# A grouped 3x3 convolution on normalised images: statistics in groups of 12 images instead of 8, measured further ahead, and 13 of 20 images in the combined form instead of 3 of 5

## The chip, the cores and the metric

The kernel runs on one core of a Trainium2 chip. The core has TensorE (matrix products, PE in the profile), VectorE (DVE), ScalarE (ACT), GpSimd (POOL) and SyncE (SP), which here only issues transfers. Each takes its own instructions strictly in order. They share the on-chip memory SBUF; TensorE writes its sums to a second memory, PSUM, in banks of 512 numbers for each of the 128 partitions. The metric is the time of one execution in microseconds (us); the kernel before takes 968.84 us (median of three).

## The reference, cut to what matters

160 images of 128 channels of 32 x 32 numbers. The output is the input plus a 3x3 convolution of the normalised input. Five sets of weights serve 32 images each.

```python
def _gn(v, G=32, eps=1e-5):                    # group norm: 4 channels of one image
    g = v.reshape(B_, G, C_ // G, H_, W_)
    m = jnp.mean(g, axis=(2, 3, 4), keepdims=True)
    s = jnp.var(g, axis=(2, 3, 4), keepdims=True)
    return ((g - m) / jnp.sqrt(s + eps)).reshape(v.shape)
...
    s1 = (beta - alpha) / RES_DENOS[0]         # beta, alpha: max and min of U
    v1 = s1 * _ste_floor(U / s1)               # the weights in two levels
    s2 = s1 / RES_DENOS[1]
    v2 = s2 * _ste_floor((U - v1) / s2)
    w = (v1 + v2).reshape(OUT_CH * N, IN_CH, K, K)
    xb = x.reshape(B // N, N * C, H, W)
    act = jax.lax.conv_general_dilated(xb, w, ..., feature_group_count=N)
...
x = x + _L0_conv_ref(_gn(x), L0_conv_U)
```

The mean and the variance are taken per image and per four channels, so every image needs two statistics before it can be normalised: the mean and 1 / sqrt(variance + eps).

## The kernel before, in words

**Numbers on TensorE.** A normalised image is split into two 16-bit parts, high and low, and both are multiplied by the weights, which are integers of at most two levels and exact in 16 bits. An image takes one of two forms.

- *Combined* (`combined(i)` true). The convolution is folded over pairs of columns, so that an image needs fewer products. VectorE and GpSimd make four combinations of the raw image as a tile `v` of 2048 numbers per partition (`combine` L681, `outer_columns` L671, `beside_pairs` L698): L687 and L694 on VectorE, L675 and L705 on GpSimd. ScalarE scales `v` by 1 / deviation to the high part `vh` (`high_combined`, L735), and VectorE makes the low part `vl` (`low_combined`, L741). TensorE then does 24 matmuls.
- *Not combined.* The image is normalised to `z` by GpSimd (L711) or, where `by_scalar_too(i)` is true, by ScalarE (`normalise`, L637). ScalarE casts it to `hi` (L645), VectorE makes the low part `lo` (L748) and combines only its rows (`combinations`, L761, L769, L770). TensorE does 30 matmuls, 18 of them on `hi` (`taps`, L785).

Which images are combined: none of the first 7, every odd one up to 29, from 30 to 129 those with `i % 5` of 0, 2 and 4, and from 130 on all but those with `i % 4` of 2.

**Statistics.** Each image is read ahead of time. ScalarE passes over it twice (`measure`): once for the sum (`image_sum`, L241) and once for the squares (`image_square`, L248). Eight early images are measured by VectorE instead (`BY_VECTOR`). Images are put in groups (`self.groups`): small ones up to 24, then 8 images each. When the last image of a group has been measured, the group goes through a chain, one step in each turn of the main loop:

1. `ready`: a small matmul with `gavg` averages the sums over four channels (`means`, L256); at the end of that turn VectorE forms the deviations with `deviations_by_vector` (L296 to L302).
2. `middle`: a second small matmul (`variances`, L273), and ScalarE scales its result to `ve` (`deviation`, L279).
3. `scaled`: GpSimd raises `ve` to the power -1/2 (`power`, L286), and VectorE scales that to `rstd` (L307) and forms `shift`, the mean times `rstd` (`scales_by_vector`, L309).

`shift` is read by ScalarE's `normalise` alone. `by_scalar_too` picks the first seven images and the first image of every group for it.

**The order.** `run` writes out the whole order by hand; no scheduler moves anything. One turn of its loop, for image i, issues in this order: TensorE's sums for image i + 1 and main products of image i (`conv`); VectorE's low part of image i + 2; on GpSimd `power` for a group in step 3, then the combinations or `z` of image i + 4 (both wait for VectorE's last instruction but one, so that they run beside the pairs); ScalarE's sum pass over the image to be measured, then its copy of image i - 1 out of PSUM (`residual`, L926), whose transfer GpSimd issues (`accumulate`, L950, added to the output in memory); ScalarE's copy of a PSUM bank for image i + 1 (`leave`, L888), its high part of image i + 3, and its square pass; on VectorE the start values of image i + 1 (`pairs`, L900 and L902), then `scales_by_vector`, then `combine` of image i + 4, then `deviations_by_vector`. Between these, VectorE and ScalarE make the next set's weights in small steps (`Later`).

**How far ahead.** Turn i measures up to image i + `min(10 + i // 4, STAT_LEAD + 1)` - 1. With `STAT_LEAD` 14 that is 14 ahead from turn 20 on.

**Transfers.** Images come in pairs into 12 buffers of two. SyncE issues a load (L495) once the buffer's former images are used up, by the rule in `consumed(c)`, and four turns later the store of the raw images to the output (L965), to which the copies out of PSUM are added later.

Of the kernel before, what the change touches and what calls it, by code (L numbers as in the profile page):

```python
# [8 lines left out]
F32 = mybir.dt.float32  # L9
I32 = mybir.dt.int32  # L10
MM = mybir.dt.float16
ALU = mybir.AluOpType
# [9 lines left out]
NB = 2  # L22
# [14 lines left out]
class Later:  # L37


    def __init__(self, steps=(), pace=0.0):  # L40
        self.steps = iter(steps)
        self.pace, self.due = pace, 0.0
        self.scalar = False
# [19 lines left out]
    def finish(self):  # L63
        run(self.steps)
# [125 lines left out]
def group_mean_matrix(nc, pool):  # L190

    P = nc.NUM_PARTITIONS
    gavg = pool.tile([P, P // GROUP, GROUP], F32, tag="gavg", name="gavg")
    nc.gpsimd.memset(gavg, 1.0 / GROUP)
    nc.gpsimd.affine_select(
        out=gavg, in_=gavg, compare_op=ALU.is_ge, fill=0.0, base=0,
        pattern=[[-GROUP, P // GROUP], [0, GROUP]], channel_multiplier=1,
    )
    nc.gpsimd.affine_select(
        out=gavg, in_=gavg, compare_op=ALU.is_ge, fill=0.0, base=GROUP - 1,  # L200
        pattern=[[GROUP, P // GROUP], [0, GROUP]], channel_multiplier=-1,
    )
    return gavg.rearrange("p g k -> p (g k)")


class Statistics:
# [5 lines left out]
    def __init__(self, nc, small, gavg, mhalf, nb, scale, name):  # L212
        self.nc, self.small, self.gavg, self.mhalf = nc, small, gavg, mhalf
        self.nb, self.scale, self.name = nb, scale, name
        self.late = False

        self.mv = self.tile("mv", [nb, 2])

# [85 lines left out]
    def scales_by_vector(self):  # L304

        vector = self.nc.vector
        vector.tensor_scalar_mul(self.rstd, self.rstd, self.scale)  # L307
        self.shift = self.tile("shift", [self.nb])
        vector.tensor_tensor(self.shift, self.ngm, self.rstd, ALU.mult)  # L309

    def scales(self):
        nc = self.nc
# [8 lines left out]
def general_path(tc, keep, steps, x, u, out):  # L321
# [8 lines left out]
    with tc.If(far > 0), ExitStack() as ctx:  # L330
# [9 lines left out]
        for n in range(N_SETS):  # L340
            un = one.tile([P, C, TAPS], F32, tag="u", name=f"g_u{n}")
            nc.sync.dma_start(un, uv[n])
            wn = one.tile([P, C, TAPS], F32, tag="w", name=f"g_w{n}")
            k1, k2 = run(steps.quantise(one, un, f"g{n}", F32))
            nc.vector.tensor_scalar_mul(wn, k1, steps.s1)
            nc.vector.scalar_tensor_tensor(wn, k2, steps.s2, wn, ALU.mult, ALU.add)
# [38 lines left out]
class Main:  # L385
# [21 lines left out]

    STAT_LEAD = 14  # L410
    LOAD_LEAD = 18
    CHUNKS = 12
    STEADY = 7
# [3 lines left out]
    EARLY = 8  # L417
    FIRST = 3
    HURRIED = (0, 2, 4, 8, 24)


    COLS = (1, 0, 2)
# [3 lines left out]
    def __init__(self, tc, ctx, keep, x, u, out):  # L426
        self.tc = tc
        nc = self.nc = tc.nc
        self.imgs, C, self.H, self.W = x.shape
        P = self.P = nc.NUM_PARTITIONS  # L430
        assert C == P and self.H * self.W == 1024
        self.per_set = self.imgs // N_SETS
        self.xv = x.rearrange("(b n) c h w -> n c b (h w)", n=N_SETS)
        self.ov = out.rearrange("(b n) c h w -> n c b (h w)", n=N_SETS)
        self.uv = u.rearrange("n (o i k) -> n o i k", o=C, k=TAPS)

        def pool(name, bufs, **kw):
            return ctx.enter_context(tc.tile_pool(name=name, bufs=bufs, **kw))

        self.const = pool("const", 1)  # L440
        self.qpool = pool("quant", 1)
        self.wpool = pool("weights", 2)
        self.upool = pool("u", 1)
        self.xpool = pool("x", self.CHUNKS)
        self.zpool = pool("z", 2)
        self.parts = pool("parts", 4)
        self.rows = pool("rows", 4)
        self.wide = pool("wide", 2)
        self.wide_parts = pool("wide_parts", 3)
        self.evac = pool("evac", 2)  # L450
        self.sums = pool("sums", 3)
        self.unread = pool("unread", 1)
        self.small = pool("small", 3)
        self.ps_eo = pool("ps_eo", 2, space=PSUM)
        ps_m = pool("ps_m", 1, space=PSUM)
        ps_small = pool("ps_small", 1, space=PSUM)
        self.steps = Steps(nc, keep)

        self.m1a, self.m1b, self.m2_ps = (
            ps_m.tile([P, self.H // 2, self.W], F32, tag=name, name=name)  # L460
            for name in ("m1a", "m1b", "m2")
        )
        self.pair = [self.m1a, self.m2_ps]

        small = ps_small.tile([P, 512], F32, tag="small", name="small")
        self.pt, self.pg = small[:, : ROW * P].rearrange("p (k o) -> p k o", k=ROW), small[:, ROW * P :]
        self.chunks, self.z, self.hi, self.v, self.eo, self.m2 = {}, {}, {}, {}, {}, {}
        self.sum, self.stored = {}, {}
        self.tables, self.wts, self.across = {}, {}, {}
        self.columns = []  # L470

        cuts = [0, 2, 4, 8, 12, 16, 20, *range(24, self.imgs + 1, 8)]
        self.groups = [range(a, b) for a, b in zip(cuts, cuts[1:])]
        self.group_of = {i: k for k, g in enumerate(self.groups) for i in g}
        self.stats = {}
# [117 lines left out]
    def keep_sums(self, n, col):  # L593
        wt = self.wts[n, col]
        run(self.both_sums(
            self.nc.gpsimd, wt[:, self.SUM], wt[:, self.DIFF], *(wt[:, k] for k in range(ROW))
        ))
# [9 lines left out]
    def stats_of(self, k):  # L607
        if k not in self.stats:
            self.stats[k] = Statistics(
                self.nc, self.small, self.gavg, self.mhalf, len(self.groups[k]),  # L610
                self.steps.lift, k,
            )
            self.stats[k].late = self.groups[k].start not in self.HURRIED
        return self.stats[k]

    def measure(self, i, stages=(0, 1)):
# [31 lines left out]
    def combined(self, i):  # L648

        if i < self.STEADY or i >= self.imgs:  # L650
            return False

        if i < self.FIFTHS:
            return i % 2 == 1
        return i % 5 % 2 == 0 if i < self.THIRDS else i % 4 != 2

    def by_scalar_too(self, i):

        return i < self.FIRST + 4 or i == self.groups[self.group_of[i]].start

    def column_of(self, i):

# [306 lines left out]

    def consumed(self, c):  # L970

        return max(i + 2 if self.by_hand(i) else i - 2 for i in range(c * NB, c * NB + NB))

    def run(self):
        nc, P = self.nc, self.P
# [26 lines left out]
        self.ident5 = self.const.tile([P, P], MM, tag="ident5", name="ident5")  # L1002
        nc.gpsimd.tensor_scalar_mul(self.ident5, ident, 5.0)
        self.gavg = group_mean_matrix(nc, self.const)
        self.mhalf = self.const.tile([P, 8], F32, tag="mhalf", name="mhalf")
        nc.gpsimd.memset(self.mhalf, -0.5)

        self.los = []
# [97 lines left out]
        for i in range(self.imgs):  # L1106
# [30 lines left out]
            else:  # L1137
                j = i - 1
                self.conv(i, on_the_way)
            ahead = i + min(10 + i // 4, self.STAT_LEAD + 1)  # L1140
            to_measure = range(measured, min(self.imgs, ahead))
# [163 lines left out]
```

## Time and profile before

| | |
|---|---|
| runs, us | 968.79, 968.84, 969.57; median 968.84 |
| profiled execution, us | 968.17 |
| its span, first to last instruction, us | 966.4 |
| TensorE clock granted | 0.998 of full |
| PE busy | 926.9 us, 96% of the span |
| VectorE busy | 910.1 us, 94% |
| ScalarE busy | 862.0 us, 89% |
| GpSimd busy | 463.6 us, 48% |
| transfers | 254.22 MB, 263 GB/s mean |

The profile shows one execution. The span is what the instructions cover; about 1.8 us lie around it, so a change of the span is a change of the profiled execution's time, and the median of the runs stands 0.67 us above that one. Lines such as L735 are lines of the kernel before. In a group of instructions the name left of the arrow is written and the names right of it are read. An instruction's duration on ScalarE or VectorE overlaps the next one by up to 0.1 us, and a matmul's by more, so that time per instruction is better read from one start to the next. After an idle stretch the profile names in brackets what ended it. The kernel's first 60 us hold the first weights; the turns of the loop after that take 4.7 to 8.4 us each.

### The profile page before, as it was taken

How to read it: one execution, taken by the hardware profiler on the slowest of the kernel's cores; microseconds unless marked ns; L12 is line 12 of the kernel's file. 1: busy time of each engine (PE TensorE's matmuls, PEld its weight loads, DVE VectorE, ACT ScalarE, POOL GpSimd, SP SyncE). 2: the span in 40 equal slices, each digit the busy share in tenths (PEclk: the TensorE clock that was granted, in tenths of full speed). 3: DMA queues.
4: the chain of work that ended last, by engine and by line, in shares of the span. 5: the costliest groups of instructions: out<-in, count | busy, mean ns of one | idle time of the engine just before them, and what ended most of it. 6: DMA issues, size and time to landing. Idle time of an engine off the chain costs nothing.

```text
span 966.4 us, 13055 instructions
## 1 busy us (share of the span) xinstructions
PE 926.9 (96%) x4432; PEld 433.6 (45%) x4432; DVE 910.1 (94%) x1280; ACT 862.0 (89%) x1167; POOL 463.6 (48%) x477
## 2 busy tenths in 40 slices
PE   2999999999999999999999999999999999999997
PEld 1444444444444444444444444444444444444443
DVE  7999999999999999989999999999999998998995
ACT  5879999999999999999989999999989999998561
POOL 4345344446445444554355435534445545666550
PEclk9999999999999999999999999999999999999999
DMA  9079999999999999999999999999999999666663
GB/s 363 20 273 340 338 328 321 334 322 315 327 320 328 314 327 323 311 315 258 283 243 287 276 305 286 278 251 301 278 274 260 286 275 255 98 90 107 91 107 112
DMA packets 67450, 254.22 MB, mean 263 GB/s; under 512 B 5296, under 2 KB 5296, under 8 KB 67376
## 3 DMA queue, kind: packets, MB, share of 16 engines
q1 hardware_dynamic: 45344, 173.09, 47.6%
q0 software_dynamic: 22032, 80.23, 44.7%
q8 instruction: 36, 0.59, 0.2%
q14 instruction: 38, 0.31, 0.1%
HBM read 89.19 MB, written 164.10 MB: 262 GB/s over the span
## 4 chain that ended last, share of the span: by engine, by line


## 5 line engine op out<-in xcount | busy, mean ns | idle before, releaser
L785 PE MATMUL eo<-hi,wt 128*128 128x496 f16 (+3 forms) x1170 | 310.3, 375 | 0.9 <-ACT wt L567 0.9
L840 PEld LDWEIGHTS <-wt 128*128 128x128 f16 x1884 | 183.9, 99 | 211.5 <-DVE rows L770 1.7
L741 DVE SCALAR_TENSOR_TENSOR vl<-v,rstd,vh 128x2048 f16<-128x2048 f32 x94 | 221.5, 2356 | 1.0 <-ACT vh L735 0.9
L840 PE MATMUL eo<-vh,wt 128*128 128x512 f16 x561 | 210.2, 375 | 0.2 <-DVE eo L902 0.2
L840 PE MATMUL eo<-vl,wt 128*128 128x512 f16 x561 | 210.1, 375 | 0.0
L735 ACT ACTIVATE vh<-v,rstd 128x2048 f16<-128x2048 f32 x94 | 188.1, 2001 | 13.4 <-DVE v L694 13.0
L926 ACT COPY sum<-eo 128x1024 f32<-128x1024 f32 x153 | 160.7, 1050 | 29.4 <-PE eo L840 28.5
L675 POOL TENSOR_SCALAR v<-xt,ngm 128x64 f32<-128x64 f32 x94 | 83.0, 883 | 215.5 <-issue 66.8
L785 PEld LDWEIGHTS <-wt 128*128 128x128 f16 x1242 | 120.9, 99 | 140.2 <-DVE eo L902 2.6
L248 ACT ACTIVATE junk<-xt,mv 128x1024 uint8<-128x1024 f32 x152 | 174.4, 1147 | 0.1
L840 PEld LDWEIGHTS <-across 128*128 128x128 f16 x1128 | 110.3, 98 | 140.3 <-issue 13.3
L241 ACT ACTIVATE junk<-xt 128x1024 uint8<-128x1024 f32 x152 | 160.5, 1056 | 13.8 <-DMA xt<-in_x_dram 10.7
L711 POOL TENSOR_SCALAR z<-xt,ngm,rstd 128x1024 f32<-128x1024 f32 x49 | 90.5, 1847 | 155.9 <-DVE rows L769 45.9
L840 PE MATMUL eo<-rows,wt 128*128 128x512 f16 x378 | 143.5, 380 | 0.0
L950 POOL DMA_DIRECT2D out_dram<-sum x153 | 133.8, 876 | 9.5 <-ACT sum L926 6.1
L840 PE MATMUL m<-vl,across 128*128 128x496 f16 (+1 forms) x282 | 105.6, 374 | 9.5 <-DVE vl L741 9.5
L687 DVE TENSOR_TENSOR v<-xt 128x960 f32<-128x960 f32 x94 | 109.0, 1160 | 0.0
L840 PE MATMUL m<-vh,across 128*128 128x496 f16 (+1 forms) x282 | 105.6, 375 | 0.9 <-ACT m L888 0.9
L888 ACT ACTIVATE m<-m 128x512 f32<-128x512 f32 x157 | 93.8, 597 | 13.4 <-PE m L840 13.2
L705 POOL TENSOR_TENSOR v<-xt 128x512 f32<-128x512 f32 x94 | 97.2, 1034 | 0.0
L748 DVE TENSOR_TENSOR lo<-z,hi 128x1024 f16<-128x1024 f32 x66 | 80.6, 1220 | 0.0
L286 POOL TENSOR_TENSOR rstd<-ve,mhalf 128x8 f32<-128x8 f32 (+2 forms) x24 | 39.1, 1629 | 68.8 <-DVE rows L769 22.0
(150 smaller groups left out, 1182.3 us busy)
## 6 DMA issues: line engine op xcount, KB each, us to landing
xt<-in_x_dram SPq DMA_DIRECT2D x78, 1024.0 KB, 12.7
out_dram<-sum POOLq DMA_DIRECT2D x153, 512.0 KB, 8.8
out_dram<-xt SPq DMA_DIRECT2D x76, 1024.0 KB, 18.6
out_dram<-xt SPq DMA_DIRECT2D x7, 512.0 KB, 3.7
u<-in_L_conv_U_dram SPq DMA_DIRECT2D x4, 576.0 KB, 19.0
xt<-in_x_dram SPq DMA_DIRECT2D x4, 512.0 KB, 9.7
range<-in_L_conv_U_dram SPq DMA_DIRECT2D x3, 576.0 KB, 7.9
u<-in_L_conv_U_dram SPq DMA_DIRECT2D x2, 288.0 KB, 3.2
```

Of the source, the lines that this page charges most:

```text
L241: self.nc.scalar.activation(junk, image, ACTF.Copy, scale=-1.0 / image.shape[1], accum_out=self.mv[:, j, 0:1],)
L248: self.nc.scalar.activation(junk, image, ACTF.Square, bias=self.mv[:, j, 0:1], accum_out=self.mv[:, j, 1:2],)
L687: nc.vector.tensor_tensor(self.view(v, 1, (511, 2), (half, H), (1, half - 1)), self.view(x, 1, (1, 2), (W, H), (2, half - 1)), self.view(x ...
L705: ins = nc.gpsimd.tensor_sub(self.v[i][:, 1536:], odd, even)
L711: ins = nc.gpsimd.tensor_scalar(z, self.image(i), st.ngm[:, j], st.rstd[:, j], ALU.add, ALU.mult)
L735: self.nc.scalar.mul(vh, self.v[i], st.rstd[:, j])
L741: yield self.nc.vector.scalar_tensor_tensor(vl, self.v[i], st.rstd[:, j], self.hi[i], ALU.mult, ALU.subtract)
L785: nc.tensor.matmul(self.bank(target, a)[:, first:end, c0:c1], self.wts[n, col][:, k, :], tile[:, s0 : s0 + 2 * (end - first) - 1 : 2, c0 + ...
L840: self.nc.tensor.matmul(out, weights, moving, start=start and j == 0, stop=False, skip_group_check=True)
L888: self.nc.scalar.mul(m2, self.m2_ps, 0.5)
L926: nc.scalar.copy(self.as_banks(i, self.sum[i]), self.flat(i, eo))
L950: added = self.nc.gpsimd.dma_start(self.ov[n, :, b], self.sum.pop(i), accum_op=ALU.add)
```

## The change

Four things.

- Groups: 8 images each up to 48, then 12 each up to 144, then two of 8. Twenty groups instead of twenty-four. The constant tile `mhalf` grows from 8 to 16 columns. `STAT_LEAD` becomes 19, so that the distance grows up to 19 images, reached at turn 40; the two agree up to turn 23. Counted from its first image, a group of 12 goes through its chain one turn earlier than a group of 8 did, and the last two groups, of 8, five turns earlier.
- `shift`: groups that start at 32 or later have none, and no image from 32 on is normalised by ScalarE; the first image of a group goes to GpSimd like the others.
- Which images are combined from 30 to 129: those with `i * 13 % 20 < 13`, 65 instead of 60.
- `consumed`: a buffer counts as used up one turn earlier.

```diff
@@ class Statistics
-        self.late = False
+        self.late = self.shifted = False
@@ def scales_by_vector
         vector.tensor_scalar_mul(self.rstd, self.rstd, self.scale)
-        self.shift = self.tile("shift", [self.nb])
-        vector.tensor_tensor(self.shift, self.ngm, self.rstd, ALU.mult)
+        if self.shifted:
+            self.shift = self.tile("shift", [self.nb])
+            vector.tensor_tensor(self.shift, self.ngm, self.rstd, ALU.mult)
@@ class Main
-    STAT_LEAD = 14
+    STAT_LEAD = 19
...
+    BY_SCALAR = 32
@@ def __init__
-        cuts = [0, 2, 4, 8, 12, 16, 20, *range(24, self.imgs + 1, 8)]
+        cuts = [0, 2, 4, 8, 12, 16, 20, 24, 32, 40, *range(48, self.imgs - 12, 12), 152, self.imgs]
@@ def stats_of
             self.stats[k].late = self.groups[k].start not in self.HURRIED
+            self.stats[k].shifted = self.groups[k].start < self.BY_SCALAR
@@ def combined
-        return i % 5 % 2 == 0 if i < self.THIRDS else i % 4 != 2
+        return i * 13 % 20 < 13 if i < self.THIRDS else i % 4 != 2
@@ def by_scalar_too
-        return i < self.FIRST + 4 or i == self.groups[self.group_of[i]].start
+        start = self.groups[self.group_of[i]].start
+        return i < self.FIRST + 4 or i == start and start < self.BY_SCALAR
@@ def consumed
-        return max(i + 2 if self.by_hand(i) else i - 2 for i in range(c * NB, c * NB + NB))
+        return max(i + 2 if self.by_hand(i) else i - 3 for i in range(c * NB, c * NB + NB))
@@ def run
-        self.mhalf = self.const.tile([P, 8], F32, tag="mhalf", name="mhalf")
+        self.mhalf = self.const.tile([P, 16], F32, tag="mhalf", name="mhalf")
```

## The prediction

> **What bounds the kernel now.** I read the page's first part, then the table of windows, the waits, and two stretches of the timeline. (The page's chain that ended last is empty here.) I call one turn of the image loop in `run` pass i.
>
> ```profile
> PE 926.9 (96%) x4432; PEld 433.6 (45%) x4432; DVE 910.1 (94%) x1280; ACT 862.0 (89%) x1167; POOL 463.6 (48%) x477
> ```
>
> Three engines stand near the span, so a mean says little. By stage (columns: PE, weight load, DVE, ACT, POOL busy us, clock, DMA share, GB/s):
>
> ```profile
> 187.00:303.00 116.00, 115.65 (x558) 54.46 (x558) 111.52 (x155) 111.62 (x154) 57.96 (x57) 1.00 1.04 320
> 303.00:412.00 109.00, 108.82 (x523) 50.95 (x522) 106.35 (x150) 106.02 (x143) 50.96 (x51) 1.00 1.04 322
> 412.00:785.00 373.00, 368.44 (x1767) 172.07 (x1766) 358.17 (x492) 354.76 (x486) 176.68 (x174) 1.00 1.01 278
> 785.00:945.00 160.00, 157.10 (x748) 73.27 (x747) 147.58 (x175) 132.95 (x160) 92.64 (x81) 1.00 0.72 136
> ```
>
> From 187 us on TensorE all but never stops; ScalarE and VectorE follow at 95 to 96% until 785. The matmuls' ends are modelled, so I checked by start times: a matmul starts every 0.21 us without a break, except in a few places. From the waits, the reason for nearly all of those:
>
> ```profile
> PE m L840 <- DVE vl L741: 9.5, 9, 1.9
> DVE rstd L307 <- POOL rstd L286: 2.9, 13, 0.2
> ```
>
> The timeline shows one of the two largest, at the moment when a group's scales are made:
>
> ```profile
> 489.54 1.84 POOL L286 TENSOR_TENSOR rstd<-ve,mhalf 128x8 f32<-128x8 f32 x1 [4.09 <-DVE rows L770]
> 490.50 0.70 DVE L902 SCALAR_TENSOR_TENSOR eo<-m1b,m 128x512 f32<-128x512 f32 x1
> 491.42 0.36 DVE L307 TENSOR_SCALAR rstd<-rstd,lift 128x8 f32<-128x8 f32 x1 [0.22 <-POOL rstd L286]
> 491.72 1.03 POOL L705 TENSOR_TENSOR v<-xt 128x512 f32<-128x512 f32 x1
> 491.82 0.97 DVE L309 TENSOR_TENSOR shift<-ngm,rstd 128x8 f32<-128x8 f32 x1
> 492.70 1.15 DVE L687 TENSOR_TENSOR v<-xt 128x960 f32<-128x960 f32 x1
> 494.61 2.00 ACT L735 ACTIVATE vh<-v,rstd 128x2048 f16<-128x2048 f32 x1 [1.93 <-DVE v L694]
> 496.83 0.38 PE L840 MATMUL m<-vl,across 128*128 128x512 f16 x1 [1.94 <-DVE vl L741]
> ```
>
> An 8-column `shift` takes 0.97 us because it ends with POOL's L705; the combination L687 is late, then `vh`, then `vl`, then TensorE. By start times TensorE loses 2.11 us here, 2.11 at 725, 1.13 at each of 816, 860 and 904, 0.84 at 466, 0.35 at 409, and crumbs: 9.1 us after 303. Before that, the last loss is ScalarE's:
>
> ```profile
> 186.68 0.62 ACT L888 ACTIVATE m<-m 128x512 f32<-128x512 f32 x1
> 187.35 0.38 PE L840 MATMUL m<-vh,across 128*128 128x512 f16 x1 [0.94 <-ACT m L888]
> ```
>
> At 187 us, in pass 24, ScalarE has no lead at all over TensorE. The new lead begins to differ in this very pass.
>
> **The Trainium skill.** "SBUF — State Buffer", section "Who interferes with whom": a VectorE instruction with two SBUF inputs contends with a GpSimd instruction that reads SBUF, and whoever starts first blocks the other. The trace agrees: `shift` takes 0.16 us alone and 0.96 beside L705, and L687 lies over L705 by more than 0.1 us only where it is itself longer. "TensorE: Matmul & The Clock Gate", "Back-to-back issue gap": it gives 216 ns for an isolated 512-column matmul and 131 ns in a stream; the trace has 0.215 us in the stream, so I use the trace. "Perfetto Trace Analysis", "Identifying the Most-Contended Engine": occupancy measures VectorE and ScalarE fairly, matmul busy time does not; hence the start times.
>
> **Five more combined images.** From 30 to 129, 65 instead of 60 are combined. A combined image has 24 matmuls: 12 go from 837.99 to 840.53, so 5.08 us. Another has 30: 1.30 (404.70 to 406.00) plus 5.10 (840.53 to 845.77 less a 0.14 statistics matmul), 6.39. TensorE saves 5 x 1.31 = 6.5 us, and it is the bound. ScalarE pays 1.90 instead of 0.94 each (start to start), +4.8. VectorE pays 2.26 + 1.07 + 0.66 = 3.99 for 1.13 + 0.60 + 2 x 0.34 = 2.41, +7.9 in all. POOL gains five pairs L675/L705, +9.6; its 49 images of L711 stay 49, since five group starts move to it.
>
> **Groups of 12.** 24 groups become 20. TensorE: 4 x 2 x 0.14 = -1.1 us. VectorE: four times 0.53 for the means and 0.27 for `rstd`, -3.2. ScalarE: five `z` of group starts, 5 x 1.27 = -6.4. The power takes 0.8 us for 2 columns, about 1.1 for 4, 1.76 for 8: for 12 I estimate 2.4, between 1.8 (all fixed) and 2.6 (in proportion). VectorE already waits for it, so +0.6 in each of eight moments.
>
> **No shift.** The row gives 16 x 0.53 = 8.5 us. I count almost nothing: where it took 0.96, L687, also with two SBUF inputs, waits in its place until L705 is over. Bounds: -0.9 and 0 us in each moment.
>
> **Where the moments fall.** Scales are made in the pass that also combines the image four ahead. Before, that was pass start - 4 and the group's first image; now it is start - 5 and image start - 1 (image 38 for the group at 40, 139 and 147 for the last two). Before, all five stalls of over 1 us came at starts 80, 120, 136, 144 and 152, the second of two combined images in a row; 40 is the one such start without a stall. Where the image stood otherwise (32, 64, 72, 104, 112) TensorE lost at most 0.35, and five starts are not combined. Now only 31 and 71 are second; 47, 59, 107, 119, 131, 139 and 147 are first in their row, 38, 83 and 95 not combined. With the longer power I take 2.7 us for 72, 0.6 for each of 48, 60, 108, 120, 132, 144 and 152, and 0.8 as at 466: 7.7 instead of 9.1. Bounds 4 (all first ones are free) and 12 (VectorE, with 3 to 4 us more work and less TensorE time to hide it, stalls at all).
>
> **Measuring further ahead.** Passes 24, 28, 32, 36 and 40 measure two images: five early pairs of 1.04 + 0.21 + 0.96 + 0.09 = 2.30 us on ScalarE, 11.5, paid back only after pass 140, where ScalarE has room anyway. ScalarE's instructions of passes 24 to 43, start to start: 20 x (0.96 + 0.48 + 2.30) = 74.8; `vh` and `hi` of images 27 to 46: 12 x 1.90 + 8 x 0.94 = 30.3; weights and small things 2.8; together 107.9, against 112.3 between the copies of images 24 (186.7) and 44 (299.0). New: 74.8 + 11.5 + 13 x 1.90 + 7 x 0.94 + 2.8 = 120.4. With no lead at 187 the copy of image 44 comes at 307.1, and TensorE, 0.6 behind, begins the sums of image 45 at 307.7 instead of 303.2: +4.5, and 0.5 for ScalarE's own waits, +5.0. Bounds +1 (the copies get ahead in ways the sum doesn't see) and +10. What is queued behind the extra pair is `sum`, then `m`, for which VectorE's L900 and then TensorE wait.
>
> Transfers must stay hidden for that:
>
> ```profile
> xt<-in_x_dram SPq DMA_DIRECT2D x6, 1024.0 KB, 30.5
> out_dram<-sum POOLq DMA_DIRECT2D x11, 512.0 KB, 8.7
> ```
>
> That is 187 to 245 us. The load of images 46 and 47 starts at 186.7, lands at 217.3 and is read at 233.9. Read in pass 30 it has about 8 us of cover instead of 16.6, images 54 and 55 about 4. The load's earlier place (`consumed`) helps little here, since SP's queue stands some 10 us behind in this stage (the load that pass 21 asks for, over at about 177, starts at 186.7), held by stores of inputs that have not landed yet; at worst it delays one store. I count 0, up to 4 if a landing slips. The wider `mhalf` is set once in the prologue: 0.
>
> **Sum.** TensorE after pass 44: of the 6.5, 1.3 lie inside the ramp, where ScalarE decides; -5.2. Statistics matmuls -1.1. Stalls 7.7 - 9.1 = -1.4. Ramp +5.0. Together -2.7 on 968.17 (profiled execution: span 966.4 and 1.8 around it): 965.5. The median of the runs lies 0.67 above it, so 966.1.
>
> **Rivals.**
> Full gain: the ramp costs 0.5. For it: VectorE had 1.41 us of idle at 242 and ScalarE 1.19 at 218, so the stage has some give. Against: ScalarE's lead of zero at 187. 966.1 - 4.5 = 961.6.
>
> Wash: VectorE becomes the second bound and stalls come to 10 or more. For it: while weights are made its instructions fill 97 to 99% of TensorE's time. 968.8.
>
> Slower: ScalarE stays the limit from pass 24 to 64 with waits of its own. Its instructions there come to 229.1 us; with 3% of waits (before it had 4% in passes 24 to 43) 236.2, against 225.4 before, +10.8. Only three images and three groups are saved after that, -4.7, and 1.5 of stalls: +4.6, 973.4. It decides once the ramp costs over 7.7 us. Against it: as the laggard it rarely waits for the others.
>
> Inert: the instruction lists have the 30 and 8 fewer matmuls, so that is excluded.
>
> **Numbers.** About 0.2%, 1.9 us, is what a measurement can tell from no change. The forecast has 0.53 (own range 963 to 969.5, of it 0.36 faster, 0.15 same, 0.02 slower), full gain 0.17, wash 0.14 (0.12 same, 0.02 slower), slower 0.16. Faster 0.53, same 0.27, slower 0.20. Range 960.5 to 972.5.
>
> **What would show it.** Right: copy of image 44 near 307, ScalarE's busy share near full from 187 to there, TensorE waiting for L888; from there the same images closer together; stalls on `vl` fewer, with L687 lengthened beside L705. Wrong: L241 waiting for a load, no wait for L888 in the ramp, or VectorE's stalls rising beyond 500 us.

## The result and the profile after

The changed kernel takes 976.18 us (median of four, 975.57 to 977.07) against 968.97 us for the kernel before beside it: a ratio of 1.0077, with a 95% interval of 1.0065 to 1.0089. It is 0.8% slower, where 966.1 us was forecast. Its profiled execution took 977.07 us with a span of 975.3, so the span grew by 8.9 us. The granted clock is 0.996 against 0.998. The lines of the changed kernel that follow L309 have numbers higher by one to four: L844 is what was L840, L745 what was L741, L892 what was L888.

The page's first part, after:

```profile
PE 923.8 (95%) x4386; PEld 427.5 (44%) x4386; DVE 910.6 (93%) x1235; ACT 862.8 (88%) x1158; POOL 478.9 (49%) x483
```

Every engine but GpSimd is busy as long as before to within 1 us, or shorter, and still the span is longer. So the change bought its work and lost more in waiting. Where, the table of windows shows (PE, weight load, DVE, ACT, POOL busy us, clock, DMA share, GB/s):

```profile
187.00:303.00 116.00, 109.01 (x521) 50.46 (x521) 107.12 (x146) 115.18 (x161) 55.28 (x54) 1.00 1.04 327
303.00:412.00 109.00, 104.58 (x496) 47.64 (x495) 104.68 (x135) 103.77 (x143) 51.73 (x52) 1.00 1.03 296
412.00:785.00 373.00, 364.80 (x1728) 168.06 (x1727) 358.14 (x466) 353.87 (x475) 188.98 (x177) 1.00 0.99 275
785.00:945.00 160.00, 160.00 (x763) 74.63 (x761) 146.44 (x169) 127.87 (x151) 95.32 (x84) 1.00 0.75 149
```

From 187 to 303 us TensorE now starts 521 matmuls where it started 558, and ScalarE has become full: 115.18 of 116. From 303 to 785 TensorE is idle more often too. Only in the last row is it better than before: it no longer stops at all. The waits, after:

```profile
PE m L844 <- DVE vl L745: 12.1, 15, 2.0
PE m L844 <- ACT m L892: 6.6, 6, 1.7
PE m L844 <- DVE rows L774: 2.8, 7, 0.8
DVE rstd L307 <- POOL rstd L286: 5.5, 8, 0.9
```

There are thus two new losses: ScalarE's in the ramp, as I call the stretch from 187 to 303 us, where the distance grows (6.6 where it was 0.9), and more of VectorE's `vl` (12.1 where it was 9.5, although the tail's three are gone).

**A ledger by start times.** As in the prediction I count what TensorE loses between the start of one matmul and the next, beyond the 0.21 us that it takes in a stream. TensorE's own work fell by 6.5 + 1.1 = 7.6 us by the prediction's counts; the losses after 187 us came to 9.0 before and 24.0 after. Together +7.4, where the spans of the two profiled executions differ by 8.9 and the medians by 7.2. The trace shows what the ledger leaves out of the spans. From 455.6 to 458.9 us the changed kernel's matmuls start 0.42 us apart instead of 0.21, eight times in a row, although TensorE waits for nothing. That is 1.6 us more. The table of windows has a granted clock of 0.59 around it, where the longer stretches above have 1.00:

```profile
454.80:459.00 4.20, 4.11 (x12) 1.56 (x12) 4.17 (x6) 4.17 (x7) 2.24 (x3) 0.59 0.93 264
```

With that the ledger has +9.0 for the 8.9. The kernel before has no such stretch in its profiled execution but in the first 30 us and the last 6, nor has e8, which is the changed kernel but for `shift`; so nothing ties these 1.6 us to the change. Why the clock fell there the record doesn't show.

The same ledger for each kernel that was run (us lost in each stretch; the median and the ratio to the kernel before beside it). It leaves out stretches at half the clock (e9 has one at 361 us as well; e4, e5, e6 and e9 have one near 41 us), and one stall of 1.1 us, ending between 187 and 189 us, that every kernel has:

| kernel | 187-303 | 303-785 | 785-945 | span | median | ratio (95%) |
|---|---|---|---|---|---|---|
| before | 0 | 5.6 | 3.4 | 966.4 | 968.97 | 1 |
| after | 7.5 | 16.5 | 0 | 975.3 | 976.18 | 1.0077 (1.0065-1.0089) |
| e1, before with 13 of 20 | 2.2 | 17.3 | 3.4 | 974.6 | 977.73 | 1.0097 (1.008-1.0113) |
| e2, after with 3 of 5 | 5.2 | 7.4 | 0 | 968.9 | 970.72 | 1.0024 (1.0014-1.0034) |
| e3, after with groups of 8 | 3.9 | 12.6 | 0 | 966.9 | 969.55 | 1.001 (1.0003-1.0017) |
| e4, after, five images unmeasured | 1.0 | 15.1 | 0 | 967.1 | 968.88 | 1.0003 (0.9994-1.0012) |
| e5, after, no scales made from 48 | 7.6 | 4.7 | 0 | 962.4 | 964.31 | 0.9955 (0.9938-0.9971) |
| e6, after, half of `vl` | 7.5 | 2.9 | 0 | 961.0 | 962.66 | 0.9934 (0.9918-0.9951) |
| e7, after, groups of 8 and 3 of 5 | 1.2 | 2.3 | 0 | 961.0 | 963.35 | 0.9947 (0.993-0.9963) |
| e8, after with all shifts | 7.5 | 17.3 | 0.3 | 974.6 | 976.83 | 1.0086 (1.0069-1.0103) |
| e9, e7 with 65 combined, spread | 5.2 | 18.5 | 0 | 976.5 | 978.29 | 1.0087 (1.0069-1.0105) |
| e10, e7 with 60 in the new order | 3.1 | 9.2 | 0 | 970.2 | 971.52 | 1.0022 (1.0013-1.003) |
| e11, before with distance 15 | 1.2 | 3.6 | 0.2 | 961.9 | 964.09 | 0.9948 (0.9932-0.9965) |

The kernel before took 968.87 us beside e1 to e4, 968.42 beside e5 to e8, and 969.29 beside e9 to e11.

**The ramp, in the timeline of the changed kernel.** ScalarE and the TensorE instruction that waits for it:

```profile
249.68 1.14 ACT L248 ACTIVATE junk<-xt,mv 128x1024 uint8<-128x1024 f32 x1
...
250.81 0.17 ACT L279 ACTIVATE ve<-small 128x8 f32<-128x8 f32 x1
250.87 0.83 ACT L134 ACTIVATE nnn<-u,s1r 128x384 int16<-128x384 f32 x1
251.60 1.05 ACT L241 ACTIVATE junk<-xt 128x1024 uint8<-128x1024 f32 x1
...
252.64 1.06 ACT L930 COPY sum<-eo 128x1024 f32<-128x1024 f32 x1
253.59 0.59 ACT L892 ACTIVATE m<-m 128x512 f32<-128x512 f32 x1
...
254.23 0.38 PE L844 MATMUL m<-vh,across 128*128 128x512 f16 x1 [1.61 <-ACT m L892]
```

ScalarE has no gap, none of its instructions carries a bracket, and TensorE waits 1.61 us for the bank that L892 empties. It is one of the six waits of that row; the others end at 188 (the one that every kernel has), 200, 235, 273 and 290 us.

**A moment, in the same kernel.** A moment is the place in VectorE's order where a group's scales are made (L307). This is the group of 96, whose scales are made beside an image that is not combined. VectorE, GpSimd's two instructions, and TensorE:

```profile
584.56 2.34 DVE L745 SCALAR_TENSOR_TENSOR vl<-v,rstd,vh 128x2048 f16<-128x2048 f32 x1
...
584.80 4.27 POOL L286 TENSOR_TENSOR rstd<-ve,mhalf 128x12 f32<-128x12 f32 x1 [1.15 <-DVE v L698]
...
589.08 1.18 POOL L715 TENSOR_SCALAR z<-xt,ngm,rstd 128x1024 f32<-128x1024 f32 x1
589.10 1.19 DVE L307 TENSOR_SCALAR rstd<-rstd,lift 128x12 f32<-128x12 f32 x1 [0.85 <-POOL rstd L286]
...
590.20 2.34 DVE L745 SCALAR_TENSOR_TENSOR vl<-v,rstd,vh 128x2048 f16<-128x2048 f32 x1
...
600.17 0.82 PE L844 MATMUL m<-rows,wt 128*128 128x512 f16 x3 [0.22 <-DVE rows L774]
...
603.10 2.35 DVE L745 SCALAR_TENSOR_TENSOR vl<-v,rstd,vh 128x2048 f16<-128x2048 f32 x1
...
605.50 0.38 PE L844 MATMUL m<-vl,across 128*128 128x512 f16 x1 [1.05 <-DVE vl L745]
```

VectorE loses 0.85 us waiting and 1.10 in L307, 1.95 together. Between 590.20 and 605.36 it has no idle of as much as 0.1 us: each instruction follows the one ahead. The delay comes out at TensorE 11 and 16 us later, as 0.38 and 1.21 us by start times. A stall and its cause do not lie in the same pass; only the row of uninterrupted VectorE instructions between them joins them.

### The profile page after: what moved, and what is told of

Read it like the earlier page. It is cut to its first block, busy times and chain, and to the rows that moved or that the text cites. A ratio compares the mean times of both kernels' runs of the same rounds, so it can differ in the third digit from the quotient of the medians.

```text
span 975.3 us, 12918 instructions
## 1 busy us (share of the span) xinstructions
PE 923.8 (95%) x4386; PEld 427.5 (44%) x4386; DVE 910.6 (93%) x1235; ACT 862.8 (88%) x1158; POOL 478.9 (49%) x483
## 4 chain that ended last, share of the span: by engine, by line
## 5 line engine op out<-in xcount | busy, mean ns | idle before, releaser
L789 PE MATMUL eo<-hi,wt 128*128 128x496 f16 (+3 forms) x1080 | 286.4, 375 | 0.7 <-ACT wt L569 0.7
L844 PEld LDWEIGHTS <-wt 128*128 128x128 f16 x1884 | 182.7, 99 | 217.1 <-DVE rows L774 6.7
L745 DVE SCALAR_TENSOR_TENSOR vl<-v,rstd,vh 128x2048 f16<-128x2048 f32 x99 | 232.1, 2345 | 1.1 <-ACT vh L739 0.9
L844 PE MATMUL eo<-vh,wt 128*128 128x496 f16 (+1 forms) x591 | 221.4, 375 | 1.2 <-DVE eo L906 1.2
L844 PE MATMUL eo<-vl,wt 128*128 128x496 f16 (+1 forms) x591 | 221.3, 375 | 0.0
L739 ACT ACTIVATE vh<-v,rstd 128x2048 f16<-128x2048 f32 x99 | 198.1, 2001 | 15.7 <-DVE v L698 15.4
L844 PEld LDWEIGHTS <-across 128*128 128x128 f16 x1188 | 116.5, 98 | 158.3 <-issue 26.6
L241 ACT ACTIVATE junk<-xt 128x1024 uint8<-128x1024 f32 x152 | 160.5, 1056 | 14.5 <-DMA xt<-in_x_dram 11.1
L715 POOL TENSOR_SCALAR z<-xt,ngm,rstd 128x1024 f32<-128x1024 f32 x49 | 104.6, 2134 | 132.9 <-DVE rows L774 26.2
L789 PEld LDWEIGHTS <-wt 128*128 128x128 f16 x1152 | 111.9, 99 | 130.7 <-DVE eo L906 3.8
L844 PE MATMUL eo<-rows,wt 128*128 128x512 f16 x348 | 132.1, 380 | 0.0
L844 PE MATMUL m<-vl,across 128*128 128x496 f16 (+1 forms) x297 | 111.5, 376 | 12.1 <-DVE vl L745 12.1
L691 DVE TENSOR_TENSOR v<-xt 128x960 f32<-128x960 f32 x99 | 119.2, 1204 | 0.0
L844 PE MATMUL m<-vh,across 128*128 128x496 f16 (+1 forms) x297 | 111.5, 375 | 6.6 <-ACT m L892 6.6
L892 ACT ACTIVATE m<-m 128x512 f32<-128x512 f32 x157 | 94.1, 599 | 14.7 <-PE m L844 14.5
L698 DVE SCALAR_TENSOR_TENSOR v<-xt,twice 128x512 f32<-128x512 f32 x99 | 73.7, 745 | 0.0
```

The costliest lines, as they stand in the source:

```text
L241: self.nc.scalar.activation(junk, image, ACTF.Copy, scale=-1.0 / image.shape[1], accum_out=self.mv[:, j, 0:1],)
L691: nc.vector.tensor_tensor(self.view(v, 1, (511, 2), (half, H), (1, half - 1)), self.view(x, 1, (1, 2), (W, H), (2, half - 1)), self.view(x ...
L715: ins = nc.gpsimd.tensor_scalar(z, self.image(i), st.ngm[:, j], st.rstd[:, j], ALU.add, ALU.mult)
L739: self.nc.scalar.mul(vh, self.v[i], st.rstd[:, j])
L745: yield self.nc.vector.scalar_tensor_tensor(vl, self.v[i], st.rstd[:, j], self.hi[i], ALU.mult, ALU.subtract)
L789: nc.tensor.matmul(self.bank(target, a)[:, first:end, c0:c1], self.wts[n, col][:, k, :], tile[:, s0 : s0 + 2 * (end - first) - 1 : 2, c0 + ...
```

## The experiments

**One part at a time.** The pattern alone on the kernel before, the pattern undone in the changed kernel, and the groups undone there.

```diff
# e1_pattern_only (kernel before)
-        return i % 5 % 2 == 0 if i < self.THIRDS else i % 4 != 2
+        return i * 13 % 20 < 13 if i < self.THIRDS else i % 4 != 2
```

> The kernel before with one part of the change: 13 of 20 images combined from 30 to 129; groups of 8, the lead of 14, shift and the buffers' rule stay. TensorE has 6.5 us less to do. Theory A (the loss is ScalarE's ramp in passes 24 to 43, about 6 us, and little else): the saving shows, 963 to 965 us. Theory B1 (VectorE can't carry five more combined images while weights are made): stalls on vl eat it, 968 to 971. Theory B2 (VectorE is held up by the longer power of groups of 12 and its place): as A, 963 to 965.

Measured: 977.73 us, 8.9 above the kernel before and above all that was expected; B1, with stalls on `vl`, came nearest. The ledger has most of the price: TensorE did 6.5 us less work, and lost 22.9 us instead of 9.0, all but some 2 us of it to `vl`.

```diff
# e2_pattern_undone (changed kernel)
-        return i * 13 % 20 < 13 if i < self.THIRDS else i % 4 != 2
+        return i % 5 % 2 == 0 if i < self.THIRDS else i % 4 != 2
```

> The changed kernel with 3 of 5 images combined from 30 to 129, as before; groups of 12, the lead of 19 and no shift stay. TensorE's work is that of before less 1.1 us, the ramp costs ScalarE the same 11.5 us. A: ramp +6, stalls as before: 974. B1: the same, 974, since VectorE has its old load. B2: the moments of the scales go on costing, TensorE stalls after 303 us of about 16 us instead of 9: 980.

Measured: 970.72 us, 5.5 less than the changed kernel. The pattern costs 5.5 us in this setting, on top of its 6.5 us less work. Losses after 187 us are halved, 24.0 to 12.6. All three theories expected more, 974 to 980.

```diff
# e3_groups_of_8 (changed kernel)
-    STAT_LEAD = 19
+    STAT_LEAD = 15
-        cuts = [0, 2, 4, 8, 12, 16, 20, 24, 32, 40, *range(48, self.imgs - 12, 12), 152, self.imgs]
+        cuts = [0, 2, 4, 8, 12, 16, 20, *range(24, self.imgs + 1, 8)]
```

> The changed kernel with groups of 8 images from 24 on and a lead of 15 instead of 19 (so that the scales are still made at start - 5); 13 of 20 combined and no shift stay. One early pair of passes on ScalarE instead of five. A: ramp cost 1 to 1.5 instead of 6, the rest saved: 964. B1: VectorE's stalls stay at about 16 us: 970 to 972. B2: power back to 1.8 us per group, stalls back to 9: 964.

Measured: 969.55 us, 6.6 less than the changed kernel. With a distance of 15 a group has its scales five turns ahead of its first image, as the groups from 48 to 132 have in the changed kernel. So groups of 12 with their longer distance cost 6.6 us here. The ledger has 3.6 of it in the ramp and 3.9 after 303, less 1.1 for the statistics matmuls. A and B2 had 964; B1's 970 to 972 came nearest.

**The ramp.** GpSimd writes constants in place of ScalarE's two passes over images 39, 44, 49, 54 and 59, those that the growing distance adds.

```diff
# e4_five_unmeasured (changed kernel)
+    UNMEASURED = (39, 44, 49, 54, 59)
+        if i in self.UNMEASURED:
+            for s in stages:
+                self.nc.gpsimd.memset(st.mv[:, j, s : s + 1], (0.0, 1024.0)[s])
+            return
```

> The changed kernel with the two ScalarE passes of images 39, 44, 49, 54 and 59 left out (GpSimd writes constants in place of their sums, so these five images and their groups are normalised with other numbers); all else stays. ScalarE has in passes 24 to 43 what it had before. A: the ramp's cost goes, 6 to 7.5 us less than the changed kernel: 969 to 970. B1 and B2: the same for this stage, with TensorE's stalls after 303 us still at 16. If ScalarE's ramp is not the limit: 976.

Measured: 968.88 us, 7.3 less than the changed kernel. Of the six waits for ScalarE's copy only the one is left that every kernel has, and the ramp's losses fall from 7.5 to 1.0; after 303 us they are nearly what they were (15.1 for 16.5). The cause of the ramp's loss is shown: five pairs of ScalarE's passes, put ahead where ScalarE has nothing to spare.

**The stalls of the main stretch.** Two kernels take away one side each: the moments (from the group of 48 on, constants stand for the scales, so neither the power nor L307 is done), or VectorE's load (it makes half of `vl`, and TensorE reads that half twice).

```diff
# e5_no_moments (changed kernel)
             self.stats[k].late = self.groups[k].start not in self.HURRIED
+            self.stats[k].fixed = self.groups[k].start >= 48
...
+        if self.fixed:      # in power
+            return self.nc.gpsimd.memset(self.rstd, 2.0**14 * 0.0023)
...
+        if self.fixed:      # in scales_by_vector
+            return
```

> The changed kernel in which groups that start at 48 or later take a constant scale: GpSimd writes it in place of the power, and VectorE's instruction on rstd is left out (so images from 48 on are scaled by a fixed number). The ten moments after 48 cost VectorE and GpSimd next to nothing; all other work stays. Theory C (each moment holds VectorE up by 1.5 to 2.3 us, and with 13 of 20 combined VectorE has no slack to make it good, so TensorE pays): stalls after 303 us fall from 16.5 to about 3, 962 to 964 us. Theory B1 (VectorE simply has too much work with five more combined images, moments or not): stalls stay above 10, 971 or more.

```diff
# e6_half_low (changed kernel)
+        w = 1024 if i >= self.FIFTHS else 2048
-            vl, self.v[i], st.rstd[:, j], self.hi[i], ALU.mult, ALU.subtract
+            vl[:, :w], self.v[i][:, :w], st.rstd[:, j], self.hi[i][:, :w], ALU.mult, ALU.subtract
...
-            source = source[:, quarter * 512 : quarter * 512 + 512]
+            q = quarter % 2 if j == 1 and i >= self.FIFTHS else quarter
+            source = source[:, q * 512 : q * 512 + 512]
```

> The changed kernel in which VectorE makes only half of vl (1024 of 2048 columns) for combined images from 30 on, and TensorE reads that half twice, so that the low part of these images is wrong for two of four combinations. VectorE has about 1.1 us less per combined image; TensorE, ScalarE, GpSimd and the moments keep all their work. Theory C and theory B1: with slack on VectorE the delays are made good, stalls on vl after 303 us nearly vanish, the ramp stays: 961 to 964. If the moments reach TensorE whatever VectorE's slack is: 974 to 976.

Measured: 964.31 and 962.66 us, 11.9 and 13.5 less than the changed kernel. The waits of TensorE for `vl`, first in e5 (where L750 is the `vl`), then in e6 (L746):

```profile
PE m L849 <- DVE vl L750: 4.7, 7, 1.4
```

```profile
PE m L846 <- DVE vl L746: 2.8, 3, 1.4
```

Both kernels do the full changed pattern on TensorE with the full ramp (7.6 and 7.5 us lost from 187 to 303). Without moments the losses from 303 to 785 fall from 16.5 to 4.7; with VectorE relieved, and every moment in its place, to 2.9. So it takes both: a moment costs TensorE something only because VectorE has nothing to spare, and VectorE's fullness costs little without moments. The moment of 84 shows it in e6: VectorE waits 0.85 us for the power and spends 1.10 in L307, as in the changed kernel, and TensorE loses nothing in the 20 us after it, where it lost 1.6. In e5 the stalls of 72, 84, 96, 108 and 120 are gone and 60's as well; of those around the moment of 48 one of 1.22 us stays, at 320 us, and one of 0.87 at 371, which thus need no moment from 48 on.

**The shift, and a combination of the rest.**

```diff
# e8_shift_kept (changed kernel)
-            self.stats[k].shifted = self.groups[k].start < self.BY_SCALAR
+            self.stats[k].shifted = True
```

> The changed kernel with shift still made for every group, though nobody reads it from 32 on. If taking shift away only moved its wait to the next instruction with two SBUF inputs, as the prediction says: 976 to 977. If the whole time of shift was saved (12 moments at 0.5 to 0.97 us, passed on to TensorE): 982 to 987.

Measured: 976.83 us against 976.18: no difference that the intervals tell apart. Leaving out the shift is worth nothing that these runs can show.

```diff
# e7_groups_8_pattern_old (changed kernel)
-    STAT_LEAD = 19
+    STAT_LEAD = 15
-        cuts = [0, 2, 4, 8, 12, 16, 20, 24, 32, 40, *range(48, self.imgs - 12, 12), 152, self.imgs]
+        cuts = [0, 2, 4, 8, 12, 16, 20, *range(24, self.imgs + 1, 8)]
-        return i * 13 % 20 < 13 if i < self.THIRDS else i % 4 != 2
+        return i % 5 % 2 == 0 if i < self.THIRDS else i % 4 != 2
```

> The changed kernel with groups of 8, a lead of 15 and 3 of 5 images combined: of the change only the missing shift, the group starts on GpSimd, the scales one pass earlier and the buffers' rule stay. TensorE's work is that of before. One early pair of passes costs 1 to 2 us. Theory C: with 3 of 5 VectorE has slack, and few moments stand at the second of two combined images; stalls 4 instead of 9: 965 to 966. Theory D (the earlier place of the moments gains nothing): 970.

Measured: 963.35 us, better than both theories had it; it beats both kernels: 0.53% below the kernel before (0.37 to 0.7%). What is left in it of the change is the place of the moments, one turn earlier, the missing shifts, the group starts on GpSimd and the earlier release of buffers. Its losses after 187 us are 3.5 us in all. The window that holds most of the stretch, for the kernel before, the changed kernel and e7:

```profile
303.00:785.00 482.00, 477.26 (x2289) 223.02 (x2288) 464.51 (x641) 460.77 (x628) 227.64 (x224) 1.00 1.02 288
```

```profile
303.00:785.00 482.00, 469.38 (x2222) 215.70 (x2221) 462.82 (x600) 457.63 (x617) 240.71 (x229) 1.00 1.00 280
```

```profile
303.00:785.00 482.00, 480.69 (x2305) 224.74 (x2304) 468.81 (x636) 460.05 (x629) 236.00 (x233) 1.00 1.01 289
```

TensorE is busy for 480.69 of 482 us in e7; the changed kernel starts 83 matmuls fewer in the same time.

**Which part of e7 it is.** One constant of the kernel before:

```diff
# e11_lead_15_only (kernel before)
-    STAT_LEAD = 14
+    STAT_LEAD = 15
```

> The kernel before with a lead of 15 instead of 14 and nothing else: shift, the group starts on ScalarE and 3 of 5 stay; the scales are made one pass earlier, beside the combination of image start - 1. If the gain of the run with groups of 8 and the old pattern (963.35 us, 5.1 below before) comes from the place of the moments: 963 to 965. If it comes from shift and the five group starts taken from ScalarE: 969 to 970.

Measured: 964.09 us, 5.2 less than the kernel before; e7 is 5.1 below its own. The constant alone gives the whole gain. Here is the same moment as the one shown in the prediction, of the group of 80, now one turn earlier; VectorE's instructions in order, and TensorE's that waits:

```profile
485.60 0.62 DVE L307 TENSOR_SCALAR rstd<-rstd,lift 128x8 f32<-128x8 f32 x1
486.26 0.17 DVE L309 TENSOR_TENSOR shift<-ngm,rstd 128x8 f32<-128x8 f32 x1
486.34 1.15 DVE L687 TENSOR_TENSOR v<-xt 128x960 f32<-128x960 f32 x1
487.41 0.74 DVE L694 SCALAR_TENSOR_TENSOR v<-xt,twice 128x512 f32<-128x512 f32 x1
488.07 1.22 DVE L748 TENSOR_TENSOR lo<-z,hi 128x1024 f16<-128x1024 f32 x1
...
494.54 2.35 DVE L741 SCALAR_TENSOR_TENSOR vl<-v,rstd,vh 128x2048 f16<-128x2048 f32 x1
...
496.94 0.38 PE L840 MATMUL m<-vl,across 128*128 128x512 f16 x1 [0.39 <-DVE vl L741]
```

After the combination comes the low part of an image that is not combined (L748), for which TensorE is not waiting, and only two turns on a `vl`. The stall is 0.39 us where it was 1.94. It is not that moments became shorter: by VectorE's wait and the time from L307 to what follows the shift, they take 0.7 to 1.5 us each from 300 to 785 in e11, and 0.3 to 1.5 in the kernel before. What is left is where they fall. (In e11 the tail's three fall as well, to 0.2 us in all.)

**Number or order.** Is it that 65 images are combined, or that they stand in the order two, one between, two, one between? e10 combines 60 in the new order; e9 combines 65 in the old order, with image 11 of every twenty added.

```diff
# e10_pairs_of_60 (from e7)
-        return i % 5 % 2 == 0 if i < self.THIRDS else i % 4 != 2
+        return i * 13 % 20 < 13 and i % 20 != 19 if i < self.THIRDS else i % 4 != 2
```

> Groups of 8, a lead of 15, no shift, and 60 combined images as before, but in the new order: 13 of 20 without i % 20 of 19. All engines have the work of the run with the old pattern (963.35 us). Theory of order: VectorE's delays reach TensorE as with 13 of 20, 967 to 970. Theory of load: with VectorE's old load they are made good, 963 to 965.

Measured: 971.52 us, where e7 is at 963.35 with as many images combined and the same groups. Its ratio is 1.0022 (1.0013 to 1.003) against e7's 0.9947 (0.993 to 0.9963), so the order alone costs 0.75%, 7 to 8 us, somewhat more than the theory of order had. VectorE isn't busier for it: 906.1 us in e10, 907.6 in e7. The ledger gives 8.8 of the spans' 9.2 us. The waits for `vl`, in e7 and then in e10:

```profile
PE m L844 <- DVE vl L745: 3.5, 6, 1.4
```

```profile
PE m L844 <- DVE vl L745: 7.5, 9, 1.3
PE m L844 <- DVE rows L774: 2.2, 4, 0.8
```

```diff
# e9_spread_plus_one (from e7)
-        return i % 5 % 2 == 0 if i < self.THIRDS else i % 4 != 2
+        return i % 5 % 2 == 0 or i % 20 == 11 if i < self.THIRDS else i % 4 != 2
```

> Groups of 8, a lead of 15, no shift, and 65 combined images as in the changed kernel, but in another order: the old 3 of 5 (i % 5 of 0, 2 and 4) and i % 20 of 11 besides, so that only one place in twenty images is denser. TensorE has 6.5 us less than in the run with groups of 8 and the old pattern (963.35 us). Theory of order (it is the rows of two combined images, one not, that leave VectorE no slack): stalls as there but for five places, 957 to 960. Theory of load (VectorE's 7.9 us more for five images eat its slack, in whatever order): 964 to 969, as with 13 of 20 (969.55).

Measured: 978.29 us, the slowest of all, a miss on every account: both theories stayed below 969. The added image closes a gap: 9, 10, 11 and 12 of each twenty are then combined, four in a row, and that is where the time goes. At images 49 to 52, in the timeline of e9 (TensorE's stalls alone):

```profile
353.44 0.82 PE L844 MATMUL m<-rows,wt 128*128 128x512 f16 x3 [1.03 <-DVE rows L774]
...
355.31 0.39 PE L844 MATMUL eo<-vh,wt 128*128 128x512 f16 x1 [0.40 <-DVE eo L906]
...
358.59 0.38 PE L844 MATMUL m<-vh,across 128*128 128x512 f16 x1 [0.57 <-ACT m L892]
...
360.81 0.59 PE L844 MATMUL m<-vl,across 128*128 128x512 f16 x1 [1.84 <-DVE vl L745]
```

With one of 0.5 us ahead of these, 5.0 us are lost by start times in 14 us, with both ScalarE and VectorE behind. The other four such places, around images 31, 71, 91 and 111, lose 2.7 to 4.0 each.

**What the order does, as an estimate.** A combined image costs VectorE 3.99 us by the prediction's rows, and 0.73 + 0.61 for its start values L904 and L906 (593.11 to 593.84 to 594.45): 5.33, where TensorE takes 5.08. One that is not combined costs VectorE 2.41 + 1.34 = 3.75, where TensorE takes 6.39. So in each combined image VectorE loses 0.25 us on TensorE, before weights and moments, and in each of the others it gains 2.64, from which the weights are paid. Between two rows of two the old order has two images that are not combined, with a single one between them; the new order has one. This fits e10 and e9, but it was argued from the sums and not measured by itself: no run moved the weights' steps, which share that spare time. A rival stands beside it: with the order, the kind of image that each moment falls beside changes too, and of the 9.2 us that e10 loses after 303 us, 8.1 come within 20 us after a moment. No run has the new order with 60 images and no moments, so the two aren't told apart. That ScalarE is behind too in e9 the estimate doesn't explain.

## Why the prediction was wrong, step by step

**What bounds the kernel.** Right. TensorE's work fell by what was counted, and the time is TensorE's work plus its losses in every one of the runs, to within about 2 us of the spans.

**Five more combined images.** The work was right, the verdict wrong. "TensorE saves 5 x 1.31 = 6.5 us, and it is the bound" held for the work; the prediction then listed VectorE's extra 7.9 us and let it lie beside TensorE, with no term in the sum but the stalls of the next step. The pattern costs 8.9 us net in the kernel before (e1), and 5.5 in the changed one (e2). From e7 to e3, where only the pattern differs, the ratios go from 0.9947 to 1.001, 6 us.

**Where the moments fall.** This is the step that failed. It took 7.7 us of stalls after 303, with bounds of 4 and 12, at prices read off the old order, and had nothing for the slack that VectorE's further work and the new order take away. 16.5 were measured. That this slack decides is what e5 and e6 show: 4.7 without moments, 2.9 with VectorE relieved.

| group | image combined with it | forecast | lost |
|---|---|---|---|
| 48 | 47, first of its row | 0.6 | 2.5 |
| 60 | 59, first | 0.6 | 2.2 |
| 72 | 71, second | 2.7 | 2.1 |
| 84, 96 | none (83, 95) | 0.8 in all | 1.6 each |
| 108, 120 | 107, 119, first | 0.6 each | 1.6, 2.3 |
| 132, 144, 152 | 131, 139, 147, first | 0.6 each | 0 |
| elsewhere | | | 2.6 |

(Sums of the losses that follow each moment within 20 us; "elsewhere" is the rest of the 16.5.) The rule "first in its row is cheap, second is dear" was read off one order and one place of the moments. In the new order, up to 785 us, firsts and even images that aren't combined cost 1.6 to 2.5 us, as much as the second of 72. Nor did it hold for the old order a turn earlier: in e11 the moment of 96, a second, loses nothing, and those of 80 and 120, firsts, lose 0.6 and 1.0. The bound of 12 was the right place to look, and what it counts as its reason, "VectorE, with 3 to 4 us more work and less TensorE time to hide it, stalls at all", is right in part: e5 and e6 show that VectorE's want of slack is one of two conditions. But its busy time rose by 0.5 us only (910.1 to 910.6), and in e10 the order costs with no more work at all. In the tail, on the other hand, moments cost nothing where 0.6 each was taken and 1.13 each was lost before. VectorE doesn't wait for the power there; e8, which keeps the shift, loses 0.3 us there in all and e11 0.2, so it is the earlier place that did most of it.

**Groups of 12.** The power was forecast at 2.4 us with bounds of 1.8 and 2.6: most take 2.3 to 2.7, and one 4.27. VectorE's wait for it was to grow by 0.6 us; it grew from 0.22 to 0.85 in each of the six moments from 372 to 785 us (5.5 us in the row of waits, with two older ones of 0.22). The price was right. What it cost TensorE was mis-sized with the step above.

**Measuring further ahead.** Right in mechanism, a little short in size. The copy of image 44 was forecast for 307.1 us and came at 307.74. But TensorE began the sums of image 45 at 309.71, not 307.7: 6.5 later than before instead of 4.5. By the ledger the ramp costs 7.5 less the 1.3 of work, 6.2, where the sum had 5.0, so this term was 1.2 us short. ScalarE's part was not: 6.5 of the 7.5 are waits for L892, and 6.5 is what e4 takes away. The other 1.0 are two waits for VectorE's tiles, at 230 and 236 us. What the forecast was to show came: ScalarE's share of 99% from 187 to 303, and L892 in the waits. Of its signs of being wrong one came too: VectorE's stalls beyond 500 us rose, from 5.5 to 8.2.

**No shift.** Right: "I count almost nothing". L691 takes 1204 ns on average, 1160 for L687 before, and e8 measures nothing.

**Transfers.** Right: L241 waits for no load in the ramp. It cost 0, as counted.

**The rivals.** The slower side was reached, but not by its own condition: ScalarE had to cost over 7.7 us in the ramp, and the ramp cost 6.2. "Wash" named the right engine, and that "stalls come to 10 or more" was right; its time of 968.8 stood for stalls just at 10. "Full gain" needed a ramp of 0.5. Two terms in the same direction, each beyond its forecast, make the miss: ramp +1.2, stalls 16.5 - 9.0 = +7.5 in place of -1.4, so +8.9. With that the sum of -2.7 becomes the ledger's +7.4.

## What to carry to other kernels

Where a second engine is at 95% of the bound's time, count what it gains or loses on the bound image by image, in the order in which they come, before counting a saving on the bound: the order of 60 equal images alone moved this kernel by 0.75%. A delay on such an engine costs the bound what the slack until the next point where the bound waits for it doesn't cover, here 11 and 16 us on, so a price read off one order of work isn't carried to another. And try the place of the periodic work by itself: one constant, a turn earlier, gave the 0.5% that the whole change did not.

## What the runs showed of the hardware

The contention of VectorE and GpSimd, which the prediction cites from the Trainium skill ("SBUF — State Buffer", "Who interferes with whom"), holds up either engine in this trace, whichever starts second. The power of 12 columns takes 2.34 us at 791 us, where only the end of a short VectorE instruction lies over it, and 4.27 when a `vl` of 2.34 us starts 0.24 us ahead of it. The scaling L307 of 12 columns on VectorE, 0.34 to 0.37 us in five of its eight moments, takes 1.19 when GpSimd's L715 starts 0.02 us ahead (both in the moment shown above), ending just after it. In the tail, a power of 8 columns, 1.7 us before, takes 3.30 and 3.50 beside a `vl`. The prediction counted the shift's lengthening in moments, but not that of L307. It doesn't come from leaving out the shift: in e8, which keeps it, L307 takes 1.19 us in the moments of 84 and 96 as well.

The clock that TensorE is granted can fall to half for a few microseconds in one execution and not in the next of nearly the same kernel, as from 455.6 to 458.9 us in the changed kernel and nowhere between 30 and 969 us in e8. Two profiles of this kernel should be compared stretch by stretch for the clock before a difference of 1.6 us is given to the change.
